# Expert masks of the last stage: from pair products on TensorE to a round trip through DRAM

## The chip, the core and the metric

The kernel runs on one core of a Trainium2 chip. The metric is the device time of one execution in microseconds (us). TensorE is called PE here, VectorE DVE, ScalarE ACT, GpSimd POOL; SP is SyncE, which issues the DMAs of this stage. The time before is 1818.81 us, the median of three runs (1818.36 to 1818.88).

## The reference, cut to what matters

Sixteen sequences of 256 tokens with 256 features go through four layers: cross attention, a mixture of experts, a second cross attention, and a gated linear attention that has a dense and a sparse part. Only the sparse part of the last one is touched:

```
e = softmax(x @ We)                      # 4 experts
_, idx = top_k(e, 1)                     # the first of equal ones
mask = one_hot(idx); rw = e * mask
q_e, k_e = q2 * rw, k2 * rw              # per expert
gk_e = gk2 * mask                        # the decay counts only the expert's own tokens
o_sparse = sum over experts of chunk_gla(q_e, k_e, v, gk_e)
```

Summed over the experts, two tokens s and t meet only if they chose the same expert. Their score is then multiplied by the product of both tokens' gates (the softmax values of their choices), and the decay between them sums the log gates of the tokens of that same expert. So for each sequence a kernel needs, from the choice, a 256 by 256 table of "same expert" (for the decay) and one of "product of the two gates if same expert, else zero" (for the scores), both cut by the causal mask.

## The kernel before

The work is done in stages over the 16 sequences (called batches, b). The change touches only the last stage, stage3_fast, and the code of its first groups, which are run between the last steps of the stage before.

The stage is written out by hand as a sequence of slots p = 0 to 63: batch b = p // 4 and quarter m = p % 4, two of the eight heads in each quarter. Every instruction of PE, DVE, ACT and POOL in the loop is tied to the order of the text, so each engine executes its instructions in the order in which the slots call them. In each slot stand, in this order: start steps, masking of the slot before (masked, second kind, n = 1, which also adds the two masked score blocks on POOL), keys and queries of the next slot (kq), middle steps, rest steps, decays of the next slot (gq with the dense mask, gz with the expert mask em), late steps, the dense score products (sc from f), their masking (at from sc), the factors f, the output of the slot before (o), the second products (sc from q and k). Dictionaries start, middle, rest, late, behind_mask, by_rows and logs say which extra step runs in which quarter; a step with offset 1 works on the next batch.

The extra steps that matter here, by quarter:

- Quarter 0: lows(b+1) makes the low-rank projections of the next batch in one PSUM bank, with the router's logits in rows 81 to 84 of its second half, copied to SBUF by DVE (low) and spread by two small DMAs (lowd, low2). route_rows turns the router's rows into token order by two PE transposes, written into an unused part of the score tile; route_logits takes the maximum of the four logits and the exponentials. outgates(b) begins the output gate, whose logits wait in the tile zs.
- Quarter 1: route_sums and, at the end, route(b+1), which normalises, finds the largest gate and its first expert, and leaves hot: for each token a vector of four with the gate at the chosen expert. norms(b-1) writes 8 KB (rms) to DRAM and reads it back spread over the partitions (r, two DMAs of 256 KB). outgates_end finishes a half of the output gate with a product on POOL (gw).
- Quarter 2: turn_hot turns hot by two PE transposes (hT), turned_hot copies it to SBUF. turn_ahead(b+2) turns 32 by 32 blocks on DVE (tile turned) and moves them by 16 DMAs into xnT, from which quarter 0 of the next batch makes lows(b+2).
- Quarter 3: pairs(b+1) multiplies hT with itself on PE (both): entry s, t is the product of the two gates if the experts are equal and zero otherwise. DVE makes em (both > 0, times dmask) and am (both times amask). steepest takes the largest of the log gates, twice. project(b-1) ends the batch before, with a DMA to the output.

PSUM of this stage: a pool of two banks in turn for all the small products, and single buffers for kq, gq, gz, o and the score tile sc. DMAs are issued by SP alone, which waits in its queue for what a DMA needs. Before the change its DMAs were not tied to the order of the text.

Of the kernel before, what the change touches and what calls it, by code (L numbers as in the profile page):

```python
# [17 lines left out]
P = 128  # L18
# [55 lines left out]
def layers(ctx: ExitStack, tc: tile.TileContext, t, out, check):  # L74
# [1544 lines left out]
    def stage3_fast(early_bank):  # L1619

        with ExitStack() as sx:
# [17 lines left out]
            def transpose(*a):  # L1639
                tc.keep_in_program_order(nc.tensor.transpose(*a))  # L1640

            halves = w1.tile([P, P], F32, tag="halves", name="halves")
            nc.sync.dma_start(out=halves, in_=t["halves"])
# [6 lines left out]

            hots = [w1.tile([P, 2, 4], F32, tag=f"hot{n}", name=f"hot{n}") for n in range(2)]

# [32 lines left out]
            def turn_ahead(b):  # L1685

                xnT[b] = of(b).tile([P, 2, S], F32, tag="xnT", name="xnT")
                y = w1.tile([P, 4, P], F32, tag="turned", name="turned")
                dve3.transpose(y.rearrange("p x d -> p (x d)"), xn[b].rearrange("p k d -> p (k d)"))
                to = xnT[b].rearrange("p k (i s) -> p (k i) s", i=2)  # L1690
                for q in range(0, P, 32):
                    for r in range(0, P, 32):
                        nc.sync.dma_start(out=to[r:r + 32, :, q:q + 32], in_=y[q:q + 32, :, r:r + 32])

            def lows(b):

                low[b] = of(b).tile([P, 2, S], F32, tag="low", name="low")
                ps = bank("low")
                for c in range(2):
                    for k in range(2):  # L1700
                        matmul(ps[:, c * S:(c + 1) * S], la[:, k, c * P:(c + 1) * P], xnT[b][:, k, :],
                                         start=k == 0, stop=k == 1)
                dve3.tensor_copy(low[b][:, 0, :], ps[:, :S])
                dve3.tensor_scalar(low[b][:, 1, :], ps[:, S:], vec[:, V_ONE:V_ONE + 1], None, ALU.add)
                lowd[b] = of(b).tile([P, S], F32, tag="lowd", name="lowd")
                nc.sync.dma_start(out=lowd[b][64:], in_=low[b][:64, 1, :])
                if b > 0:
                    nc.sync.dma_start(out=low2, in_=low[b][64:, 1, P:])

            e_, den_, z_ = {}, {}, {}  # L1710

            def route_rows(b, ps):

                for i in range(2):
                    transpose(ps[:, 64 * i:64 * i + 64], low[b][64:P, 1, tokens(i)], ident[64:P, 64:P])
                z_["rt"] = ps

            def route_logits(b):

                ps = z_.pop("rt")  # L1720
                src = ps.rearrange("p (i e) -> p i e", i=2)[:, :, 17:21]
                mx = st.tile([P, 2], F32, tag="emx", name="emx")
                dve.tensor_reduce(mx, src, AX.X, ALU.max)
                e = e_[b] = st.tile([P, 2, 4], F32, tag="e", name="e")
                dve.tensor_tensor(e, src, bc(mx, [P, 2, 4], 2), ALU.subtract)
                act.activation(e, e, AF.Exp)

            def route_first(b):
                route_rows(b, bank("rt")[:, :P])
                route_logits(b)  # L1730

            def route_sums(b):
                den = den_[b] = st.tile([P, 2], F32, tag="eden", name="eden")
                dve.tensor_reduce(den, e_[b], AX.X, ALU.add)
                dve.reciprocal(den, den)

            def route(b):
                e, shape = e_.pop(b), [P, 2, 4]
                dve.tensor_tensor(e, e, bc(den_.pop(b), shape, 2), ALU.mult)
                m, q, c = (st.tile(x, F32, tag=n, name=n) for n, x in (("em", [P, 2]), ("eq", shape), ("ec", [P, 2])))  # L1740
                dve.tensor_reduce(m, e, AX.X, ALU.max)
                first = bc(prio[:, 4:], shape, 1)
                dve.tensor_tensor(q, e, bc(m, shape, 2), ALU.is_equal)
                dve.tensor_tensor(q, q, first, ALU.mult)
                dve.tensor_reduce(c, q, AX.X, ALU.max)
                dve.tensor_tensor(q, q, bc(c, shape, 2), ALU.is_equal)
                dve.tensor_tensor(hots[b % 2], q, e, ALU.mult)

# [32 lines left out]

            def turn_hot(b):
                ps = bank("hT")
                for i in range(2):
                    transpose(ps[:4, tokens(i)], hots[b % 2][:, i, :], ident)
                z_[b, "hot"] = ps

            def turned_hot(b):
                hT[b] = of(b).tile([4, S], F32, tag="hT", name="hT")
                dve3.tensor_copy(hT[b], z_.pop((b, "hot"))[:4, :S])  # L1790

            def pairs(b):

                x, both = hT.pop(b), bank("both")
                matmul(both[:, 0:S], x[:, :P], x, start=True, stop=True)
                matmul(both[:, S:3 * P], x[:, P:], x[:, P:], start=True, stop=True)
                em[b] = of(b).tile([P, 2, P], F32, tag="em", name="em")
                dve3.scalar_tensor_tensor(em[b], both.rearrange("p (i s) -> p i s", i=2)[:, :, :P], 0.0, dmask,
                                          ALU.is_gt, ALU.mult)
                am[b] = of(b).tile([P, 384], F32, tag="am", name="am")  # L1800
                dve3.tensor_tensor(am[b], both[:, :384], amask, ALU.mult)

# [108 lines left out]
            def products(p, n):  # L1911

                b, m, cols = place(p)
                q, k = fq.pop((p, n)), fk.pop((p, n))
                ps = psa.tile([P, 2, 512], F32, tag="sc", name="sc")
                if n == 0 and m == 0 and b + 1 < B:
                    route_rows(b + 1, ps[:, 1, 384:])
                for lo, hi, i in ((0, S, 0), (P, S, 1)):
                    for j in range(2):
                        r = slice(64 * j, 64 * j + 64)  # L1920
                        matmul(ps[:, j, lo + i * P:hi + i * P], k[r, tokens(i)], q[r, lo:hi],
                                         start=True, stop=True)
                z_[p, n, "sc"] = ps
# [66 lines left out]
            def norms(b):  # L1990
# [8 lines left out]
                act3.activation(y, y, AF.Exp, scale=-0.5)  # L1999
                nc.sync.dma_start(out=rms[b], in_=y[0:P:16, :])  # L2000
                r = z_[b, "r"] = w1.tile([P, 4, S], F32, tag="r", name="r")
                for j in range(2):
                    nc.sync.dma_start(out=r[64 * j:64 * j + 64],
                                      in_=bc(rms[b].rearrange("(m j) s -> j m s", j=2)[j], [64, 4, S], 0))
# [6 lines left out]
            def project(b):  # L2011
                ps = bank("proj")
                for i in range(2):
                    for m in range(4):
# [3 lines left out]
                                               ALU.mult, ALU.add)  # L2018
                nc.sync.dma_start(out=out[b].rearrange("(c p) d -> p c d", p=P), in_=xs[b])

# [3 lines left out]
            def project_part(b, i, h):  # L2024
# [4 lines left out]
                if h == 1:  # L2029
                    dve3.scalar_tensor_tensor(xs[b][:, i, :], pp[i][:, :D], gate[:, 3:4], xs[b][:, i, :],  # L2030
                                              ALU.mult, ALU.add)
                    nc.sync.dma_start(out=out[b, tokens(i)], in_=xs[b][:, i, :])

            def warm():

                ps = bank("warm")
                for _ in range(2):
                    matmul(ps, ones, v[B - 1][:, 0, :], start=True, stop=True)


            start = {3: [(pairs, 1)]}
            middle = {0: [(lows, 1)], 1: [(all_gates, 1)], 2: [(turn_hot, 1)], 3: [(scaled_first, 0)]}

            rest = {0: [(bias, 2)], 1: [(route_sums, 1)], 2: [(turned_hot, 1), (norm_ahead, 2)], 3: [(steepest, 1, 0), (steepest, 1, 1)]}
            late = {1: [(norms, -1)], 2: [(vals, 1), (turn_ahead, 2)], 3: [(project, -1)]}
            behind_mask = {0: [(route_logits, 1)]}
            by_rows = {0: [(outgates, 0)], 1: [(gates_end, 1)]}
            logs = {0: [(outgates_exp, 0, 1, act3.copy), (outgates_end, 0, 0)],
                    1: [(route, 1), (stats, 2), (outgates_end, 0, 1), (gate_logs, 1, 0)],
# [10 lines left out]
            for group in (((bias, 0), (stats, 0)), ((norm, 0),), ((turn, 0),), ((lows, 0),), ((gates, 0, 0),),  # L2060
                          ((gate_logs, 0, 0), (route_first, 0)), ((route_sums, 0), (gates, 0, 1)),
                          ((route, 0), (vals, 0), (gate_logs, 0, 1), (bias, 1))):
# [4 lines left out]
            keys_queries(0)  # L2067
            for f, *a in ((turn_hot, 0), (turned_hot, 0), (stats, 1), (pairs, 0), (norm, 1), (steepest, 0, 0),
                          (steepest, 0, 1)):
                f(*a)  # L2070
# [185 lines left out]
```

## Time and profile before

| what | value |
|---|---|
| median of three runs | 1818.81 us |
| the profiled execution | 1819.15 us |
| its span, first to last instruction | 1817.4 us |
| last stage, from about | 1226 us to the end |
| mean granted TensorE clock | 0.999 |
| matmuls hT from hot, in the loop | 30, 5.7 us busy |
| matmuls both from hT, in the loop | 60, 16.1 us busy |
| transposes of the router's rows, in the loop | 30, 5.0 us busy |

One execution is profiled; its span and what lies around it (1.75 us) make its time. In the lines that follow the numbers ahead of the engine's name are the start and the length in us, counted from the start of the span; a bracket holds the idle time of the engine before the line and who ended it. In a table by stretches each engine has its busy time and its number of instructions, then follow the granted clock, the mean busy share of the 16 DMA engines, and GB/s. Line numbers such as L50 or L1637 are those of helpers through which all instructions of a kind go, so operations are told apart by the names of their tiles. Matmuls are pipelined, and the ends of their lines are modelled.

### The profile page before, as it was taken

What the parts mean: (1) busy time and instruction counts of PE and PEld (TensorE: products, weight loads), DVE (VectorE), ACT (ScalarE), POOL (GpSimd) and SP (SyncE); (2) the same over time, 40 slices, a digit from 0 to 9 for tenths busy, and PEclk for the clock granted to TensorE, in tenths of its full rate; (3) what the DMA queues carried; (4) which work ended last, traced back from release to release, by engine and by line L of the source; (5) the groups of instructions that cost most, each with busy time, mean ns of one, the idle gap of its engine ahead of it and who ended that gap; (6) DMA issues with size and microseconds to landing.
All of it is one profiled execution on the core that took longest, in us unless ns stands there. A gap on an engine that the chain in (4) does not pass through costs nothing.

```text
span 1817.4 us, 35425 instructions
## 1 busy us (share of the span) xinstructions
PE 1787.7 (98%) x13930; PEld 1240.0 (68%) x13930; DVE 1129.3 (62%) x2679; ACT 839.1 (46%) x1743; POOL 1014.9 (56%) x1001
## 2 busy tenths in 40 slices
PE   8999999999999999999999999999999999999997
PEld 5666666666666676666777866657777777777775
DVE  3345656666656666566466378876666666666664
ACT  4433345344443344433343378754554455445542
POOL 3655776567756767557552766414454445444533
PEclk9999999999999999999999999999999999999999
DMA  9800010000010000000058942200111111111110
GB/s 298 240 1 23 16 36 13 28 17 16 31 35 10 29 18 13 27 23 20 10 165 283 233 93 45 35 3 12 26 41 36 29 27 41 36 29 27 41 29 27
DMA packets 110361, 98.05 MB, mean 54 GB/s; under 512 B 43835, under 2 KB 97763, under 8 KB 109673
## 3 DMA queue, kind: packets, MB, share of 16 engines
q1 hardware_dynamic: 97897, 78.91, 14.7%
q0 software_dynamic: 12288, 16.79, 4.6%
q8 instruction: 112, 1.84, 0.4%
q14 instruction: 64, 0.52, 0.1%
HBM read 52.03 MB, written 38.41 MB: 50 GB/s over the span
## 4 chain that ended last, share of the span: by engine, by line
PE 85%; POOL 7%; DVE 4%; ACT 2%; issue 1%; DMA 0%; POOLq 0%; SPq 0%; DVEq 0%; ACTq 0%
PE o L50 11%; PE qk L50 11%; PE v L50 9%; PE sc L50 8%; PE proj L50 7%; PE kq L1637 7%; PE sc L1637 6%; PE gq L1637 4%; POOL es L50 4%; PE ex L50 3%; PE v L1637 3%; PE proj L1637 3%; PE o L1637 3%; POOL rs L50 2%; PE gz L1637 2%; PE low L1637 2%
## 5 line engine op out<-in xcount | busy, mean ns | idle before, releaser
L50 POOL TENSOR_SCALAR rs<-mv 128x2 f32<-128x2 f32 (+2 forms) x85 | 16.2, 190 | 398.3 <-DVE mv L50 388.5
L50 DVE RECIPROCAL rd<-o 128x256 f32<-128x256 f32 x64 | 112.3, 1755 | 164.2 <-PE o L50 123.8
L50 ACT ACTIVATE e<-sc 128x1024 f32<-128x1024 f32 (+1 forms) x192 | 181.5, 1015 | 18.5 <-PE sc L50 18.5
L50 POOL TENSOR_TENSOR at<-at,at 128x768 f32<-128x768 f32 x63 | 114.3, 1815 | 133.8 <-DVE at L50 133.7
L50 PE MATMUL sc<-qk 64*128 64x256 f32 (+1 forms) x1536 | 183.1, 384 | 0.5 <-DVE qk L50 0.5
L50 PE MATMUL o<-e,v 128*32 128x256 f32 (+1 forms) x3072 | 177.9, 379 | 0.0
L50 PEld LDWEIGHTS sc<-qk 64*128 64x128 f32 (+1 forms) x1536 | 132.0, 172 | 55.1 <-issue 26.8
L50 POOL TENSOR_TENSOR esum<-esum,es 128x512 f32<-128x512 f32 x128 | 163.3, 1276 | 10.0
L50 PE MATMUL qk<-kvT,wkv 128*128 128x333 f32 x512 | 164.3, 443 | 0.0
L50 POOL TENSOR_TENSOR es<-e 128x1024 f32<-128x1024 f32 x64 | 151.3, 2365 | 12.0 <-ACT e L50 9.0
L50 ACT ACTIVATE qk<-qk 128x256 f32<-128x256 f32 x128 | 48.7, 380 | 231.9 <-PE qk L50 231.9
L50 POOL TENSOR_TENSOR es<-es,e 77x1024 f32<-77x1024 f32 x64 | 150.3, 2349 | 5.0
L50 PEld LDWEIGHTS o<-e,v 128*32 128x32 f32 (+1 forms) x3072 | 99.9, 110 | 66.3
L50 PE MATMUL qk<-kvT,wq 128*128 128x256 f32 x512 | 134.6, 385 | 0.0
L50 DVE TENSOR_TENSOR at<-sc,amask 128x768 f32<-128x768 f32 x64 | 61.3, 958 | 108.6 <-PE sc L1637 82.5
L50 DVE COPY qk<-qk 128x333 f32<-128x333 f32 x128 | 64.5, 504 | 93.9 <-ACT qk L50 92.8
L50 POOL DMA_INDIRECT x<-rows_out,pos x64 | 101.3, 1582 | 35.9 <-issue 18.0
L50 PEld LDWEIGHTS qk<-kvT,wq 128*128 128x128 f32 x512 | 94.3, 189 | 35.2 <-issue 9.6
L50 PEld LDWEIGHTS qk<-kvT,wkv 128*128 128x128 f32 x512 | 97.2, 190 | 30.0
L50 PE MATMUL proj<-wo0h,oT 128*128 128x256 f32 x512 | 113.7, 380 | 0.3 <-DVE oT L50 0.3
L50 PE MATMUL v<-wkv,kvT 128*128 128x512 f32 x256 | 113.1, 595 | 0.0
L50 PEld LDWEIGHTS proj<-wo0h,oT 128*128 128x128 f32 x512 | 95.9, 190 | 13.9 <-issue 0.8
(268 smaller groups left out, 3914.4 us busy)
## 6 DMA issues: line engine op xcount, KB each, us to landing
rows<-zero SPq DMA_DIRECT2D x16, 640.0 KB
xin<-rows SPq DMA_DIRECT2D x16, 640.0 KB
r<-rms SPq DMA_DIRECT2D x30, 256.0 KB
rows_out<-y SPq DMA_DIRECT2D x16, 384.0 KB
v<-vctx SPq DMA_DIRECT2D x15, 308.0 KB
x<-in_x_dram SPq DMA_DIRECT2D x16, 256.0 KB
rows_out<-y SPq DMA_DIRECT2D x16, 256.0 KB
out_dram<-x SPq DMA_DIRECT2D x15, 256.0 KB
```

Of the source, the lines that this page charges most:

```text
L50: x = getattr(self.engine, name)(*a, **k)
L1637: tc.keep_in_program_order(nc.tensor.matmul(*a, **k))
```

## The change

The choice is no longer carried as a hot vector through PE. Four parts:

- The router's rows are turned on DVE (one transpose of 32 partitions by 256, straight from the PSUM bank of lows into the tile that turn_ahead uses). The small softmax then runs on 32 partitions with 8 by 4 values each, in place of 128 with 2 by 4. route writes the largest gate and a number for its first expert into a 32 by 32 tile, transposes that, and writes 16 rows of it to DRAM (picks: 256 gates and 256 expert numbers).
- Two DMAs read picks back: rows, 512 numbers to every one of the 128 partitions, into a buffer shared with the output gate's zs (with xn for batch 0), and cols, for each partition the gate and the number of its own two tokens, single elements of 4 bytes. same builds em from them by two DVE operations of 128 by 128; weights builds am by four, two for each half.
- The transposes on PE (route_rows, turn_hot), the copy of hT and the pair products are gone. All DMAs of the loop are tied to the order of the text.
- One of the two sums of largest gates (steepest) moves from quarter 3 to quarter 2; the first half of outgates_end moves from the end of quarter 0 to the middle of quarter 1, which puts its POOL product behind the masked sum. For batch 0 em and am are made behind the statistics and both steepest steps, and norm(1) behind them.

```
-            hots = [w1.tile([P, 2, 4], F32, tag=f"hot{n}", name=f"hot{n}") for n in range(2)]
+            choice, chosen = (w1.tile([P, 32], F32, tag=n, name=n) for n in ("choice", "chosen"))
+            nc.gpsimd.memset(choice, 0.0)
...
-                        nc.sync.dma_start(out=to[r:r + 32, :, q:q + 32], in_=y[q:q + 32, :, r:r + 32])
+                        sp.dma_start(out=to[r:r + 32, :, q:q + 32], in_=y[q:q + 32, :, r:r + 32])
...
+                rl[b] = w1.tile([P, 4, P], F32, tag="turned", name="rl")[:, :2, :].rearrange("p x d -> p (x d)")
+                dve3.transpose(rl[b][64:96, :], ps[64:96, S:])
...
-                for i in range(2):
-                    transpose(ps[:, 64 * i:64 * i + 64], low[b][64:P, 1, tokens(i)], ident[64:P, 64:P])
...
+                w, c = choice[own_rows, :8], choice[own_rows, 8:16]
...
+                dve.tensor_reduce(w, e, AX.X, ALU.max)
...
                 dve.tensor_reduce(c, q, AX.X, ALU.max)
-                dve.tensor_tensor(q, q, bc(c, shape, 2), ALU.is_equal)
-                dve.tensor_tensor(hots[b % 2], q, e, ALU.mult)
+                dve.transpose(chosen[own_rows], choice[own_rows])
+                sp.dma_start(out=picks[b].rearrange("n (k a) -> (n k) a", a=32), in_=chosen[64:80])
+                x = w2.tile([P, 512], F32, tag="zs", name="rows") if b else w0.tile([P, 2, D], F32, tag="xn", name="rows")
+                rows[b] = x.rearrange("p (n s) -> p n s", n=2) if b else x
+                sp.dma_start(out=rows[b], in_=bc(picks[b], [P, 2, S], 0))
+                cols_[b] = w1.tile([P, 2, 2], F32, tag="cols", name="cols")
+                sp.dma_start(out=cols_[b], in_=picks[b].rearrange("n (i p) -> p n i", p=P))
...
-                matmul(both[:, 0:S], x[:, :P], x, start=True, stop=True)
-                matmul(both[:, S:3 * P], x[:, P:], x[:, P:], start=True, stop=True)
...
+            def same(b):
+
+                em[b] = of(b).tile([P, 2, P], F32, tag="em", name="em")
                 for i in range(2):
-                    transpose(ps[:4, tokens(i)], hots[b % 2][:, i, :], ident)
...
+                    dve3.scalar_tensor_tensor(em[b][:, i, :], rows[b][:, 1, tokens(i)], cols_[b][:, 1, i:i + 1],
+                                               dmask[:, i, :], ALU.is_equal, ALU.mult)
+
+            def weights(b):
+
+                w, c = (rows[b][:, n, :] for n in range(2))
+                x = am[b] = of(b).tile([P, 384], F32, tag="am", name="am")
+                for i, (lo, hi) in enumerate(((0, S), (S, 3 * P))):
+                    dve3.scalar_tensor_tensor(x[:, lo:hi], c[:, i * P:], cols_[b][:, 1, i:i + 1], w[:, i * P:],
+                                               ALU.is_equal, ALU.mult)
+                    dve3.scalar_tensor_tensor(x[:, lo:hi], x[:, lo:hi], cols_[b][:, 0, i:i + 1], amask[:, lo:hi],
+                                               ALU.mult, ALU.mult)
...
-            start = {3: [(pairs, 1)]}
-            middle = {0: [(lows, 1)], 1: [(all_gates, 1)], 2: [(turn_hot, 1)], 3: [(scaled_first, 0)]}
+            start = {3: [(same, 1)]}
+            middle = {0: [(lows, 1)], 1: [(outgates_end, 0, 0), (all_gates, 1)], 3: [(scaled_first, 0)]}
...
+            rest = {0: [(bias, 2)], 1: [(route_sums, 1)], 2: [(norm_ahead, 2), (steepest, 1, 0)], 3: [(steepest, 1, 1), (weights, 1)]}
...
-            logs = {0: [(outgates_exp, 0, 1, act3.copy), (outgates_end, 0, 0)],
+            logs = {0: [(outgates_exp, 0, 1, act3.copy)],
...
+            for f, *a in ((stats, 1), (steepest, 0, 0), (steepest, 0, 1), (same, 0), (weights, 0), (norm, 1)):
```

## The prediction

> **What bounds the kernel now.** I read the page's engine table first, then the busy time by stretches of the last stage, then its timeline by engine, the DMA queue's own timeline, and the DMA share in half-microsecond stretches.
>
> ```profile
> PE 1787.7 (98%) x13930; PEld 1240.0 (68%) x13930; DVE 1129.3 (62%) x2679; ACT 839.1 (46%) x1743; POOL 1014.9 (56%) x1001
> ...
> core 0: us, PE busy (x) PEld busy (x) DVE busy (x) ACT busy (x) POOL busy (x), PEclk, DMA share, GB/s
> 1570.00:1606.20 36.20, 36.18 (x251) 26.63 (x249) 23.52 (x59) 17.95 (x43) 17.68 (x18) 1.00 0.15 33
> 1606.20:1642.40 36.20, 36.18 (x250) 26.63 (x248) 23.52 (x59) 17.94 (x43) 17.66 (x18) 1.00 0.15 33
> ```
>
> The last stage repeats every 36.2 us (the pairing matmuls start at 1579.36 and again at 1615.60: 36.24), one batch per period, and PE is busy for 36.18 of each, at full granted clock. DVE has 12.7 us free, ACT and POOL 18 each. A PE instruction that goes shortens the period by its start-to-start cost, as long as nothing else is late. Four slots make a period. These pieces of one period show what PE would lose:
>
> ```profile
> 1594.61 0.14 PEld L1640 LDWEIGHTS sc<-ident,low 64*128 64x128 f32 x1 [0.21 <-DVE low L50]
> ...
> 1607.15 1.03 PE L1637 MATMUL kq<-xnT,wq 128*128 128x256 f32 x4
> 1608.02 0.38 PE L1640 MATMUL hT<-ident,hot 128*4 128x128 f32 x2
> 1608.23 0.61 PE L1637 MATMUL gq<-dmask,lg 128*128 128x128 f32 x4
> ...
> 1615.60 0.92 PE L1637 MATMUL both<-hT 4*128 4x256 f32 x4
> 1616.44 1.13 PE L1637 MATMUL kq<-xnT,wk 128*128 128x256 f32 x4
> 1616.55 0.42 DVE L50 SCALAR_TENSOR_TENSOR em<-both,dmask 128x256 f32<-128x256 f32 x1 [0.96 <-PE both L1637]
> 1618.72 0.61 PE L1637 MATMUL gz<-em,lg 128*128 128x128 f32 x4
> ```
>
> The reader should take starts here, not durations: matmuls overlap, and the start of the next group says what one costs. The queue that the new path uses, and the transfer ahead of it:
>
> ```profile
> 1605.21 0.61 SPq L2000 DMA_DIRECT2D rms<-rs  x1
> 1606.96 1.34 SPq L2003 DMA_DIRECT2D r<-rms  x2
> 1611.90 11.56 SPq L1693 DMA_DIRECT2D xnT<-turned  x16
> 1623.63 0.47 SPq L2019 DMA_DIRECT2D out_dram<-x  x1
> ...
> 1608.00:1608.50 0.50, 0.50 (x6) 0.46 (x5) 0.50 (x4) 0.18 (x1) 0.09 (x1) 1.00 0.24 23
> 1610.50:1611.00 0.50, 0.50 (x3) 0.26 (x2) 0.00 (x0) 0.50 (x2) 0.50 (x1) 1.00 0.37 70
> ```
>
> A small write to DRAM (rms) is issued at 1605.21 and its reader at 1606.96: 1.75 us. The 512 KB of r move between about 1608.2 and 1610.9 (DMA share, last column but one). And one pair of lines from the first stage, needed for a rival:
>
> ```profile
> 190.17 2.35 POOL L50 TENSOR_TENSOR es<-es,e 77x1024 f32<-77x1024 f32 x1
> ...
> 191.30 1.25 DVE L50 TENSOR_TENSOR re<-turned,rmx 128x16 f32<-128x16 f32 x1
> ```
>
> **What PE loses.** (a) The pair products: 1615.60 to 1616.44, 0.84 us. (b) The two transposes of the hot rows: in slot 2 the last kq to gq is 1.08 us (1607.15 to 1608.23), in slot 3 without them 0.87 (1581.17 to 1582.04): 0.21. (c) The two transposes of the router's rows: PE stood 0.18 waiting for DVE's low (gz begins at 1593.99 and takes 0.45, the next start is 1594.62). The transposes themselves run partly beside sc matmuls; between 0 and 0.20 (two starts of 0.1) remains for them. I take 0.20 for all of (c), nearest to the wait that is seen, with ends 0.18 and 0.38. Sum 1.25 us a period (1.23 to 1.43), 15 periods: 18.8 us (18.5 to 21.5). The transposes of batch 0 lie in stage 2, where PE is also nearly full (171.55 of 176 us): 0.2 more.
>
> **What DVE gains and loses.** Gone per period: the hT copy 0.40, em 0.43, am 0.55, two small route operations 0.33, 1.7 us in all. New: a 32-partition transpose of 256 columns (row dens<-den, 128x256: 0.44), one of 32x32 (row turned<-rt, 128x64: at most 0.24), two 128x128 products for em (row at<-sc,kden,am: 0.34 each), four for am (2 x 0.47 + 2 x 0.34): about 3.0 us. So +1.3 us on 23.5, in a period of 35. By places: the 0.44 follows low in slot 0 (1594.56) and ends at 1595.0. Queued behind it are the masking, which waits for sc until about 1595.4 anyhow, and, on PE, the bank of low, which the zg matmuls want at about 1595.3: hidden by 0.3 us. The moved sum of largest gates (1.16) runs in slot 2 from about 1609.5 to 1610.7, where the hT copy stood; the next DVE operation, the transpose behind xn, waits for ACT until 1611.13: hidden, by 0.4. In slot 3 DVE no longer waits 0.96 for PE. It runs em (0.5), masking (1.38), u (0.68), one gate sum (1.16), then am. The next thing due is x<-proj at 1621.97 (1622.82 less the 0.84). Counting from 1616.2, am is done at about 1621.5 to 1622.0: hidden, barely; this is the tightest place.
>
> **The output gate behind masking.** POOL did gw at 1600.71 to 1601.97 and then at to 1603.75, for o on PE at 1604.10. The reverse lets at start when DVE is done (1600.08), so it ends near 1601.9, and gw near 1603.2, ahead of k at 1604.10. The matmuls were not stopped there, so I give nothing for it. Without it o would keep 0.35 us of cover. It also frees the buffer that the rows use, long before they are read.
>
> **The DRAM path and what SP queues behind it.** SP's DMAs of this stage already ran in the order of the text (the lines above), so tying them costs nothing; what is new stands between r and the block copies. SP now does rms, r, r, then picks, rows, cols, then the 16 block copies, then the output. The chosen experts are ready at about 1607.3 (route starts at 1606.09, six operations 0.2 apart). SP is free at 1608.30. The write takes 1.75 us if the engines are idle (1610.05); behind r it cannot move before 1610.9, so about 1611.4. Rows issues then (0.65, as one r), moves at +1.25 for 1.1 us (half of r) and lands at 1614.1. Cols issues at 1612.05; its 512 single elements are the unknown price. At the price of a block-copy piece (0.21 share x 0.7 us x 16 engines / 128 pieces = 18 ns) they take 0.6 us of 16 engines; at that of r's 1 KB pieces (2.25 us for 512) 2.25 us. It lands at 1614.9 to 1616.4; I take 1615.1, since its pieces are as short as the block copy's. DVE reaches em at 1615.6, and PE needs em at 1617.87 (1618.72 less 0.84): the landing may be as late as 1617.2. The Trainium skill, DMA: Bandwidth & Descriptors, section Rules for kernel authors, says that a last dimension that isn't contiguous becomes one descriptor per element; by it cols is 512 pieces, and no trace of before shows pieces of 4 bytes.
>
> The block copies start at about 1612.7 in place of 1611.90 (1613.4 at worst), take 11.56, and the last one lands 1.75 after its issue: 1625.4 to 1626.1. The low matmuls read them at 1628.05, in the new time 1627.0 (1.05 of the 1.25 falls before). Hidden by 0.9 to 1.6 us.
>
> **The prologue.** em of batch 0 was ready at 1225.81. Now DVE does x, the statistics and both gate sums (2.33) first, then em: about 1226.4. PE stood 0.7 us before and would stand longer: +0.4 us (between -1, if the 1.05 us of (a) and (b) that go count in full, and +3, if the rows land late).
>
> **Sum.** 1819.15 (the profiled execution: span 1817.4 and 1.75 around it) - 18.8 - 0.2 + 0.4 = 1800.5. The median of the runs, 1818.81, is 0.34 lower; I leave the sum as it stands.
>
> **Rivals.** First, SP's line is late (the other side). SP stands still until picks has landed, with rows, cols and 16 block copies behind. The matmuls of low pay as soon as the line slips 1.6 us past my estimate, and the gain is gone at 1.6 + 1.25 = 2.9 us, that is when the write takes 6 us and not 3.1. For it: it queues behind 512 KB, and DRAM latency is seen only for an idle queue. Against: every row of the queue is at most 1.75 us plus the transfer ahead. With 4 us late, 2.4 us x 14 = 34 less 18.6: 1834.
>
> Second, DVE against POOL. The DVE line at 191.30, 16 elements wide with both inputs in SBUF, ended 0.03 us after POOL's 2.35 us operation did; the same size takes 0.17 elsewhere. The new em and am products have both inputs in SBUF; the old had one in PSUM. em would wait for POOL's u (until 1616.13: in my count), am for at and k (until 1620.65, am done at 1622.0). If also the four products and POOL's alternate badly, DVE is 0.7 us late at x<-proj, and so at masking, where PE has 0.1 us (DVE done 1624.71, sc at about 1624.9): 0.6 x 15 = 9 us, 1809.5. The Trainium skill, SBUF — State Buffer, section Who interferes with whom, says that a DVE instruction with two SBUF inputs and a GpSimd one that reads SBUF shut each other out for a whole instruction; the trace agrees (1.25 us for 16 elements).
>
> Third, the shorter PE line uncovers another engine's chain, such as ACT's exponentials in slot 1 (the weight load of sc waits 0.5 us there for lg, 7.3 us over 15 periods). Against: that chain starts from a PE matmul and moves with it. Half the gain is 9.4: 1810.
>
> **How the numbers follow.** Forecast 0.70 (its own range 1797 to 1804), DVE against POOL 0.11, another chain 0.06, SP's line 0.13 (of which 0.03 costs only the gain). What a measurement tells from no change is 0.2%, 3.6 us. Faster 0.86, same 0.03, slower 0.11. Low 1796.5 is all of (c) and a prologue gain (21.5 + 0.2 + 1 = 22.7); high 1812 takes in the second and third rival, and about 0.15 stays outside.
>
> **What would show it.** Right: periods of 35.0 us with PE still full; no hT, both or router transposes; em on DVE starting before kq of slot 3 and no DVE wait for a DMA longer than 0.5 us; the first block copy about 4.4 us after r's issue ended (1612.7 less 1608.3). Wrong: PE low waiting for a DMA of xnT, PE gz waiting for DVE em, or DVE products of 128x128 longer than 0.6 us with sc waiting for DVE behind them.

## The result, and the profile after

The changed kernel took 1804.08 us, median of four runs (1803.20 to 1804.92), against 1818.85 for the kernel before on the same chip (also the median of four, one of which took 2297.38 and does not count in the ratio): ratio 0.992 (0.990 to 0.9939). The forecast was 1800.5, with a range of 1796.5 to 1812. So the direction was right and the time lies inside the range, but the changed kernel gained 14.8 us where 18.3 were forecast from the median.

The profiled execution took 1804.92 us, with a span of 1803.0. Lines of its page and trace: the engine table, then two stretches of one period each, measured from one write of low to the next (columns as before: busy time of each engine, granted clock, DMA share, GB/s).

```profile
PE 1771.7 (98%) x13802; PEld 1227.0 (68%) x13802; DVE 1168.2 (65%) x2727; ACT 842.4 (47%) x1743; POOL 1018.9 (57%) x1002
...
1551.83:1586.79 34.96, 34.96 (x243) 25.72 (x242) 25.75 (x61) 18.13 (x43) 17.89 (x18) 1.00 0.18 42
1586.79:1621.75 34.96, 34.96 (x243) 25.70 (x242) 25.71 (x61) 18.14 (x43) 17.90 (x18) 1.00 0.17 42
```

PE is still full, and the period went from 36.24 to 34.96 us. That is 1.28 less, where 1.25 was forecast. The queue of SP and the places that the forecast spoke of, in the timeline of the second of these periods:

```profile
1597.21 0.61 SPq L50 DMA_DIRECT2D rms<-rs  x1
1598.95 1.32 SPq L50 DMA_DIRECT2D r<-rms  x2
1600.37 0.55 SPq L50 DMA_DIRECT2D picks<-chosen  x1
1604.81 0.34 SPq L50 DMA_DIRECT2D rows<-picks  x1
1605.20 0.43 SPq L50 DMA_DIRECT2D cols<-picks  x1
1605.73 10.34 SPq L50 DMA_DIRECT2D xnT<-turned  x16
...
1608.33 0.62 DVE L50 SCALAR_TENSOR_TENSOR em<-rows,cols,dmask 128x128 f32<-128x128 f32 x2 [0.97 <-DMA cols<-picks]
1609.64 0.61 PE L1637 MATMUL gz<-em,lg 128*128 128x128 f32 x4
1611.89 0.54 DVE L50 SCALAR_TENSOR_TENSOR am<-rows,cols 128x256 f32<-128x256 f32 x1
1612.10 0.92 POOL L50 TENSOR_TENSOR k<-e,ee 128x256 f32<-128x256 f32 x1
1612.47 0.83 DVE L50 SCALAR_TENSOR_TENSOR am<-am,cols,amask 128x256 f32<-128x256 f32 x1
```

The path through DRAM is just in time. em waits 0.97 us for cols here; its two products are through at about 1608.95, and PE starts gz, which reads em, at 1609.64: 0.7 us remain.

The time came from, and was lost again at, these places (after less before, all between writes of low in the two profiled executions):

| stretch | before | after | difference |
|---|---|---|---|
| start to the write of low of batch 0 | 1204.25 | 1204.49 | +0.24 |
| the opening: to the write of batch 1 | 30.68 | 33.75 | +3.07 |
| to the write of batch 15 | 504.60 | 488.73 | -15.87 |
| from there to the end | 77.87 | 76.03 | -1.84 |
| span | 1817.4 | 1803.0 | -14.4 |

The opening is what went wrong. The granted clock was 1.00 there before (PE busy 2.00 of 2.00 us in each stretch from 1228 to 1234), for example:

```profile
1230.00:1232.00 2.00, 2.00 (x16) 1.49 (x9) 1.66 (x5) 0.50 (x1) 0.23 (x2) 1.00 0.00 0
```

After, in the timeline and then in the table by stretches:

```profile
1222.24 0.38 SPq L50 DMA_DIRECT2D cols<-picks  x1
1225.47 0.61 DVE L50 SCALAR_TENSOR_TENSOR em<-rows,cols,dmask 128x128 f32<-128x128 f32 x2
1225.88 0.75 PE L1637 MATMUL gz<-em,lg 128*128 128x128 f32 x4 [2.26 <-DVE em L50]
1231.96 2.08 PE L1637 MATMUL kq<-xnT,wk 128*128 128x256 f32 x4
...
1228.00:1230.00 2.00, 2.00 (x9) 1.18 (x8) 2.00 (x4) 0.77 (x2) 0.56 (x1) 0.61 0.00 0
1230.00:1232.00 2.00, 2.00 (x13) 0.86 (x13) 0.36 (x1) 0.97 (x2) 0.00 (x0) 0.50 0.04 8
1232.00:1234.00 2.00, 2.00 (x9) 1.64 (x6) 0.79 (x3) 0.00 (x0) 1.00 (x2) 0.50 0.00 0
1234.00:1236.00 2.00, 2.00 (x8) 1.65 (x7) 0.00 (x0) 0.00 (x0) 0.44 (x1) 0.68 0.00 0
1236.00:1238.00 2.00, 2.00 (x15) 1.84 (x13) 0.66 (x2) 0.21 (x1) 0.00 (x0) 1.00 0.00 0
```

PE waits 2.26 us for em of batch 0. Some 2.6 us after that wait the granted clock falls to 0.50 and stays there until about 1235; the group kq<-xnT,wk takes 2.08 us in place of the 1.13 that it takes in the later periods.

### The profile page after: what moved, and what is told of

It reads as the page before. It is cut to its first block, busy times and chain, and to the rows that moved or that the text cites. A ratio compares the mean times of both kernels' runs of the same rounds, so it can differ in the third digit from the quotient of the medians.

```text
span 1803.0 us, 35245 instructions
## 1 busy us (share of the span) xinstructions
PE 1771.7 (98%) x13802; PEld 1227.0 (68%) x13802; DVE 1168.2 (65%) x2727; ACT 842.4 (47%) x1743; POOL 1018.9 (57%) x1002
## 4 chain that ended last, share of the span: by engine, by line
PE 83%; POOL 7%; DVE 5%; issue 1%; ACT 1%; DMA 1%; SPq 0%; POOLq 0%; DVEq 0%; ACTq 0%
PE o L50 12%; PE qk L50 11%; PE v L50 9%; PE sc L50 8%; PE proj L50 7%; PE kq L1637 6%; PE sc L1637 6%; PE gq L1637 4%; POOL es L50 4%; PE o L1637 3%; PE ex L50 3%; PE proj L1637 3%; PE v L1637 3%; PE gz L1637 2%; POOL rs L50 2%; PE low L1637 2%
```

## The experiments

They ran on three chips, on which the kernel before took 1822.57, 1821.08 and 1822.63 us (medians); so ratios are compared, or kernels of one chip. These medians are mixtures. Of the 39 executions of the kernel before on these chips, those with a mean granted clock of 0.999 took 1818.58 to 1820.50 us, those with 0.996 took 1822.70 to 1825.23. The three of the first chip (1818.36 to 1818.88) are like the former, and only one like these was traced; where the others lost clock is not known. So small differences between ratios prove little, and the traces have to decide. The theory to be tested had three parts: the period is PE's and fell by what PE lost; the opening is lost to the clock, after a wait that the landing of cols causes; and the two periods that were longer than the others (35.96 and 35.30) are late landings of cols behind r's transfer. The rivals were DVE's order in the opening, DVE or POOL as the bound, and SP's queue.

**Is the period PE's?** Two matmuls of the shape of the pair products put back in quarter 3; nobody reads their result.

```
 em[b] = of(b).tile([P, 2, P], F32, tag="em", name="em")
+if b > 0:
+    both, x = bank("both"), low[b][:4, 0, :]
+    matmul(both[:, 0:S], x[:, :P], x, start=True, stop=True)
+    matmul(both[:, S:3 * P], x[:, P:], x[:, P:], start=True, stop=True)
```

> The changed kernel with the PE work of the pair products put back: in quarter 3 two matmuls of the same shape (4 rows, 256 and 128 columns), in the same place, on data that lies ready, and with a result that nobody reads. If PE sets the period and the start-to-start cost is the price: 0.84 us a period, 35.8 us, 12.6 us in all, less what the late landings of cols cost before, since em has 0.84 us more cover: +11.3 to +12.6 against the changed kernel. If the period were set by another engine or by the queue, much less.

1816.66 us, against 1805.73 for the changed kernel on the same chip: 10.9 more, a little under the 11.3 to 12.6 expected (ratio to before 0.9977, 0.9968 to 0.9987; the changed kernel there 0.9916, 0.9902 to 0.9929). The usual period is 35.80 us, 0.84 more:

```profile
1615.24 0.92 PE L1637 MATMUL both<-low 4*128 4x256 f32 x4
1616.08 1.13 PE L1637 MATMUL kq<-xnT,wk 128*128 128x256 f32 x4
```

The start-to-start cost of the group, 1616.08 less 1615.24, is the 0.84 that the period grew by. Term (a) is shown. That the remaining 0.44 of 36.24 - 34.96 - 0.84 belongs to (b) and (c), forecast at 0.41 together, is read from PE's starts; no run puts these back.

**What delays the opening: DVE's order or the landing?** em put between the two sums of largest gates.

```
-... (steepest, 0, 0), (steepest, 0, 1), (same, 0), (weights, 0), ...
+... (steepest, 0, 0), (same, 0), (steepest, 0, 1), (weights, 0), ...
```

> One edit against the changed kernel: for batch 0 em is made between the two gate sums and not behind both, so DVE is free for it 1.16 us sooner. The changed kernel takes 1804.1 us (median); there PE stood 2.26 us for this em and then ran at half clock from about 1228.3 to 1235.6 us. If DVE's order made em late: em starts at about 1224.3 in place of 1225.5, PE stands 1.1 us, the clock stays at 1.0, and the time is about 1801. If the landing of cols made it late (in the loop em starts 3.1 us after cols is issued; here cols is issued at 1222.24, so 1225.3): DVE waits for cols instead, em starts within 0.3 us of where it did, and the time stays at 1804 (1803.3 to 1804.8).

1806.83 us, ratio 0.9913 (0.9896 to 0.993): no gain in the time, which says little here because the clock fell once more than in the changed kernel (below). The trace says more. DVE came sooner and then waited itself:

```profile
1224.27 0.38 SPq L50 DMA_DIRECT2D cols<-picks  x1
1227.51 0.61 DVE L50 SCALAR_TENSOR_TENSOR em<-rows,cols,dmask 128x128 f32<-128x128 f32 x2 [1.25 <-DMA cols<-picks]
1227.91 0.75 PE L1637 MATMUL gz<-em,lg 128*128 128x128 f32 x4 [2.25 <-DVE em L50]
```

em began 3.24 us after cols was issued, and 3.23 in the changed kernel, where DVE arrives at the same moment. So the landing sets it, and the second sum, which stands ahead of em in the changed kernel, costs nothing. PE's wait stayed at 2.25 us and the clock fell behind it again.

**Is it the wait or the clock that costs?** Matmuls of 128 by 512 that nobody reads, ahead of batch 0's decays: two, and in another run one.

```
 keys_queries(0)
+fill = bank("fill")
+for _ in range(2):        # range(1) in the second run
+    matmul(fill, ones, v[0][:, 0, :], start=True, stop=True)
 for f, *a in ((stats, 1), (steepest, 0, 0), ...
```

> One edit: two matmuls of 128x512 whose result nobody reads are put on PE ahead of batch 0's first decays, 1.8 us of work in the 2.26 us in which PE waits for em. Nothing that the kernel needs starts sooner. If the lost time of the opening is the clock that follows the wait: the clock stays at 1.0 through 1226 to 1240 us and the time falls by about 2.7 us to 1801.4. If it is only the wait for em: the time stays at 1804 or rises by up to 0.3 us.

> The changed kernel with one 128x512 matmul that nobody reads ahead of batch 0's decays (two took 2.24 us, so one takes about 1.1 and leaves a gap of about 1.1 us ahead of gz). My theory: it is the length of the gap that halves the clock, 2.26 us does and 1.1 does not: clock 1.00 from 1222 to 1240, 30.4 us from the first to the second write of low as with two, 3 to 4 us less than the changed kernel, ratio 0.989 to 0.990. Rival: any idle stretch of over 1 us here is too long: clock 0.5 again for some 6 us, ratio 0.991 to 0.993.

With two 1801.75 us, ratio 0.9888 (0.9871 to 0.9904); with one 1804.33, ratio 0.9906 (0.9888 to 0.9923), both on chips on which the unaltered changed kernel was not run. In the traces, one execution of each, the opening took 30.39 and 30.58 us in place of 33.75, and the clock stayed at 1.00. With two:

```profile
1228.00:1230.00 2.00, 1.53 (x9) 1.02 (x10) 1.97 (x6) 1.22 (x4) 0.80 (x1) 1.00 0.00 0
1230.00:1232.00 2.00, 2.00 (x17) 1.06 (x16) 1.78 (x5) 1.50 (x4) 0.00 (x0) 1.00 0.04 8
```

With one:

```profile
1226.26 0.75 PE L1637 MATMUL gz<-em,lg 128*128 128x128 f32 x4 [1.45 <-DVE em L50]
```

The wait for em is not shortened by the fill, PE only does useless work in it, and yet the 3 us come back: the clock is the cause, not the wait itself. In the traces a wait of 1.45 us here was harmless, and with those of 2.09 us and more half the clock always came, for 6.8 or 10.2 us; in four runs it began while PE still waited, in the others behind the wait. Every trace of the new path without the fill shows the fall, with openings of 33.5 to 36.1 us. The Trainium skill, TensorE: Matmul & The Clock Gate, section What's actually happening, says that the clock halves after an idle window of about 3.4 us; here a wait of 2.26 us was enough, so the measurement decides.

The length of one wait is not a safe measure, however. In the run with em sooner the clock also fell earlier in the opening, behind a wait of only 0.90 us, with one of 0.31 us shortly before it:

```profile
1209.78 3.58 PE L50 MATMUL proj<-wo,oT 128*128 128x256 f32 x8 [0.90 <-DVE oT L50]
1209.96:1213.37 3.41, 3.41 (x12) 2.20 (x15) 2.99 (x2) 1.15 (x4) 0.00 (x0) 0.50 0.02 5
```

PE has these two waits in all 14 traces, the one of before included, and in the other 13 the clock stays at 1.00 behind them. The half-clock stretches of the openings lasted 3.41 us (this one), 6.83 us (five) or 10.24 us (five), whole multiples of 3.41 us, and the two of this run began 20.48 us apart, six times 3.41. So the clock changed in steps of 3.41 us. Laid over the traces as a raster, the eight steps in which PE stood 1.95 us or more were all followed by a fall, none with 1.19 us or less was, and of those between (1.21 to 1.72 us; PE's ends are modelled, so these sums are rough) three were and others were not. How a wait falls on the raster therefore counts beside its length, and that is luck: the 2.26 us of the changed kernel were split over two steps.

The executions that were not traced agree. With two fills all four had a mean clock of 0.997 to 0.999. With one, two took 1802.17 and 1802.55 us at 0.998 and 0.999, and two took 1806.11 and 1806.77 us at 0.995 and 0.996, so one fill does not hold the clock every time.

**Can the landing be had sooner?** First, r's two reads put behind rows and cols (queue: rms, picks, rows, cols, r, r).

```
 sp.dma_start(out=rms[b], in_=y[0:P:16, :])
+def spread(b):            # called behind route, with b - 1
     r = ...
-1: [(route, 1), (stats, 2), ...
+1: [(route, 1), (spread, -1), (stats, 2), ...
```

> One edit: the two DMAs that read r (512 KB) move behind picks, rows and cols in SP's text, so the write of picks has an idle queue ahead of it. If the late landing of cols is 512 KB of r ahead of the write: the write is read 1.75 us after its issue in place of 3.4 to 4.4, em no longer waits for a DMA (8.8 us in total before), the periods of 35.3 and 36.0 us among those of 34.96 go, and the time falls by 0.5 to 1.3 us, to 1802.8 to 1803.6. r lands later, at about 1606 in the period whose u starts at 1605.8: POOL may wait up to 0.5 us, in front of 2 us in which it has nothing to do. If the write is slow by itself: same waits, 1804.

1808.31 us, ratio 0.9921 (0.9899 to 0.9942): no gain. From the issue of picks to that of rows it took 1.36 to 1.40 us in the loop (2.2 in two periods) in place of 3.3 to 4.4, and em no longer waited; but now POOL waited for r, and periods of 35.7 to 35.8 us appeared. The waits of the whole last stage (total, times, longest):

```profile
POOL u L50 <- DMA r<-rms: 26.5, 15, 3.7
```

Then the better order: only the small write goes ahead of r (rms, picks, r, r, rows, cols).

```
 sp.dma_start(out=picks[b]..., in_=chosen[64:80])
+def route_read(b):        # rows, cols
+1: [(route, 1), (spread, -1), (route_read, 1), (stats, 2), ...
```

> One edit: in SP's text the write of picks moves ahead of the two reads of r, and rows and cols stay behind r: rms, picks, r, r, rows, cols. The write meets an idle queue and lands while r is issued. The run with r behind everything took the wait off em but put it on u, which waited 26.5 us for r, with periods of 35.7 us left. If what is late is only whatever comes last in the line, this order leaves neither late: picks lands by r's end of issue, rows is issued about 2.3 us sooner than in the changed kernel, em waits for no DMA, u for less than 2 us in all, all periods 34.96 but the first, and the time falls by 1.3 us against the changed kernel (0.0007). If the long periods come from a slow rms or r (a write that takes 3.4 and not 1.75 us, as in one period of the changed kernel), they stay, and the time is the same within 0.4 us.

1805.97 us, ratio 0.9916 (0.9903 to 0.993); the changed kernel on that chip took 1805.73 with the same ratio. The trace, though, shows the loop cured and the opening worse. From picks to rows it took 1.84 to 2.85 us, em waited for cols nowhere in the loop, and of the 13 later periods 12 are within 0.03 of 34.96, one 35.31. Against the changed kernel on that chip, whose longest period was 36.58, this saves about 2 us. The opening took 34.99 us against 33.49, because the clock fell sooner and for longer (10.24 us, not 6.83). How deep that loss is differs from run to run, and it can hide a gain of this size.

With a fill of one matmul and the keys of batch 0 moved into the wait as well, both gains show:

```
+for m in range(0, 3, 2): ... keys_ahead(0, n, ...)      # from behind decays(0)
+fill = psa.tile([P, 2, 512], F32, tag="sc", name="fill")
+matmul(fill[:, 0, :], ones, v[0][:, 0, :], start=True, stop=True)
 decays(0)
```

> The order of the run with picks first, and the opening mended: the three matmuls for the first keys of batch 0 (k) stand ahead of its decays and not behind them, and one matmul of 128x512 that nobody reads fills most of the rest of the wait for em. Expected by the filling run: the clock stays at 1.0 and some 3.1 us go against the changed kernel; another 0.5 to 1.0 us because k no longer follows em; 0 to 1.3 us from the order. Together 3.6 to 5.4 us below the changed kernel, ratio to before about 0.9895.

1800.78 us (1799.84 to 1800.95), ratio 0.9888 (0.9873 to 0.9903), the fastest version here: about 5 us below the changed kernel on the same chip (1804.10 to 1807.51). Its opening took 30.15 us at a clock of 1.00.

**How near is SP's line to the edge?** picks copied a second time through DRAM.

```
-sp.dma_start(out=picks[b]..., in_=chosen[64:80])
+sp.dma_start(out=first[b]..., in_=chosen[64:80])
+sp.dma_start(out=picks[b]..., in_=first[b]...)
```

> One edit: picks is written to one place in DRAM, copied from there to a second, and read from the second: one more trip in SP's line, some 2 us, ahead of rows, cols and the 16 block copies. It measures what cover is left. In the changed kernel em ends 0.7 us before gz needs it, and has waited 0.97 us for cols: so 2 us more should stop PE for about 1.3 us in each of 14 periods, 1804 + 18 = 1822, slower than before the change. The prediction's count (2.1 us of cover from the estimate of the landing to the point where PE pays, of which the landing as measured has used about 1.4) says the same to within 0.5 us a period. The rival, that the landing is well covered and the two long periods come from elsewhere: 1804 to 1808.

1826.65 us, ratio 1.0025 (1.0013 to 1.0037), slower than before the change. Waits of the last stage:

```profile
DVE em L50 <- DMA cols<-picks: 38.4, 15, 4.0
...
PE gz L1637 <- DVE em L50: 12.2, 15, 4.1
```

em waited 2.6 us at the mean, where it was 0.7 in the changed kernel, and PE waited for em in the opening and in all later periods but one. One more short DMA on this path takes away the whole gain. The first rival was real; the change stops short of it by less than 1 us.

**The parts that were forecast at nothing.** Three runs undo one of them each: the output gate ahead of masking again, both sums of largest gates in quarter 3 again, and SP's DMAs not tied.

```
-1: [(outgates_end, 0, 0), (all_gates, 1)]       # e9: back into quarter 0's logs
-2: [(norm_ahead, 2), (steepest, 1, 0)]          # e10: back into quarter 3
-sp = Pinned(tc, nc.sync)                        # e11
+sp = nc.sync
```

> The changed kernel, with the output gate of the first slot ahead of masking's second product on POOL again, as in the kernel before. My theory: in the changed kernel POOL does at (1592.53 to 1594.34), gw (to 1595.58), and k at 1596.09 after 0.51 us of waiting for ACT, so the order of the two does not reach PE: ratio to the kernel before as the changed kernel's, 0.991 to 0.993, periods 34.96 us. Rival: o on PE has no cover left (it had about 0.35 us before) and waits for the later at: up to 0.9 us a period, 12 us, ratio 0.998.

> The changed kernel, with both sums of largest gates in slot 3 again, as in the kernel before. My theory: DVE runs without a gap from em to the next masking there (em 1608.33, x<-proj 1613.87, masking 1614.68), so 1.21 us more makes masking 1.2 us late, PE's sc had about 0.1 us of cover: periods of 35.5 to 36.1, 8 to 16 us more than the changed kernel, sc on PE waiting for DVE at every time. Rival: DVE catches up before PE needs it (it has 2.08 us free ahead of the next low): periods 34.96, no change.

> The changed kernel, with SP's DMAs of the last stage not tied to the order of the text. My theory: they ran in that order in the kernel before too, so nothing changes: ratio 0.991 to 0.993, within 1 us of the changed kernel. Rival: without the tie another order of picks, r and the block copies comes out, and waits of em for cols (8 to 12 us in all in the changed kernel) go or grow by more than 5 us.

They took 1809.61, 1813.90 and 1812.02 us, with ratios of 0.9928 (0.9914 to 0.9941), 0.9956 (0.9939 to 0.9972) and 0.994 (0.9927 to 0.9954); the changed kernel had 0.9916 and 0.992 on two other chips. These intervals overlap or touch, so the periods have to decide. The usual one is 35.13, 35.23 and 35.22 us against 34.96: about 0.17, 0.27 and 0.26 more, a loss of 2.4 to 3.8 us over 14 periods; untied, four are 36.0 to 36.8 long, where the changed kernel has one of 35.96. None of the three parts was free. I compared PE's starts, group by group from the write of low, with those of the changed kernel, in a usual period of each. In the first, everything agrees up to the output products of the first slot, o, which start 0.17 later; the weight loads show why:

```profile
1599.89 0.63 PEld L1637 LDWEIGHTS o<-at,v 128*64 128x64 f32 x8 [0.29 <-POOL at L50]
```

In the other two the first differences are 0.17 at the sc products of the last slot and 0.27 at den behind them. With both sums back, PE's wait there is for masking:

```profile
1586.96 0.73 PEld L1637 LDWEIGHTS sc<-q,k 64*128 64x128 f32 x8 [0.41 <-DVE at L50]
```

Untied, a block copy slipped in ahead of the reads. SP stood there until DVE had made the tile turned, and rows was issued 4.84 us after picks, 3.3 to 4.4 in the changed kernel:

```profile
1606.89 0.55 SPq L1745 DMA_DIRECT2D picks<-chosen  x1
1610.59 0.64 SPq L1695 DMA_DIRECT2D xnT<-turned  x1
1611.73 0.34 SPq L1748 DMA_DIRECT2D rows<-picks  x1
1612.12 0.42 SPq L1750 DMA_DIRECT2D cols<-picks  x1
```

em waited 24.1 us for cols in all, against 8.8 in the first run of the changed kernel and 11.9 in its second. DVE then came late to the same masking as with the sums.

## Why the prediction was right, and where it was wrong

- **What bounds it, and (a), (b), (c).** Right. 1.25 us a period was forecast and 1.28 measured; the pair products are 0.84 by the trace and by putting them back. (b) is 0.21: kq to gq in quarter 2 takes 0.87 now, 1.08 before. (c) fell from gz to o by 2.46 - 2.26 = 0.20, the value taken.
- **The prologue.** This is the step that failed: "+0.4 us" was worked out, with a range of up to +3, and the opening took 3.07 longer. The prediction put em's start down to DVE's order. In fact cols' landing sets it, 3.2 us after its issue, as moving em showed. It then counted PE's wait as lost time at one price. PE's wait lasted 2.26 us, and its larger cost was the clock behind it: with PE kept busy the opening took 30.4 us, 0.3 less than before the change. That 3.07 lies near the range's upper end is luck: +3 was given for a late landing, which by the runs with the fill cost nothing by itself.
- **The DRAM path.** Right that it fits, wrong in the write's size. "About 1611.4", 3.1 us from the issue of picks to that of rows, is 3.3 to 4.4 in the trace. In the period shown, cols' issue to em took 3.13 us, against 3.05 by the price of a short piece (1612.05 to 1615.1). So the block copies began 5.5 us after r's issue ended, not 4.4, em waited 0.97 and not under 0.5, and it started 0.96 us behind kq of slot 3 (1607.37), not before it. None of this reached PE in the usual period. In one period it did: the write of rms took 3.36 us from issue to its reader (1526.29 to 1529.65) in place of 1.75, picks and cols followed late, and em waited 2.18. That period took 35.96 us; the section on the hardware shows what stood in the way.
- **The sum.** From the profiled execution 18.6 us were forecast and 14.2 came. The opening accounts for 2.9 of the missing 4.4 (3.07 less the 0.2 of its forecast, 0.4 - 0.2), the period of 35.96 for 1.0, and one of 35.30 for 0.3. The comparison is with an execution of the kernel before that kept its clock; one of those at 0.996 would have left a larger gain. The 35.30 is there in nearly every run of the new path, the one without waits for cols too; what makes it I have not found.
- **DVE against POOL.** The mechanism was there and the price small. am's products took 0.54 and 0.83 us where POOL's k, 0.92 in place of 0.73, ran beside them, against 0.48 each in the opening. In the usual period PE did not wait for masking; in five places it did, 3.4 us in all (before in two, 1.4 us). The Trainium skill, SBUF — State Buffer, section Who interferes with whom, says that a DVE instruction with two SBUF inputs contends with a GpSimd one that reads SBUF; these rows agree in that all three operations got longer. They were not shut out for their whole length, as the forecast had it: 0.48, 0.73 and 0.48 us make 1.69, and the three were through in 1.41 (1611.89 to 1613.30).
- **The moved gate sum, the output gate and the queue's order.** "I give nothing for it" and "tying them costs nothing" are right as costs but miss what the parts do. Each keeps 0.17 to 0.27 us a period that the shorter PE line would otherwise lose to POOL, DVE or SP. The cover of 0.35 us that o was said to keep was counted in the old period. In the run with the gate back, POOL's at ended 9.41 us after the write of low (9.16 before the change), while o would start at 9.30 (9.51 before).
- **DVE's margin in slot 3.** "hidden, barely; this is the tightest place" was right, although DVE's busy time rose by 2.2 us a period (23.52 to 25.71) and not by 1.3. My later expectation for the sums put back, 0.5 to 1.1 us a period, was too high: 0.27. With the sums later, am no longer ran beside POOL's k (0.47 and 0.48 us), and part of the delay was taken up by slack ahead of masking.

## What to carry to other kernels

When a full engine's line gets shorter, every part that was hidden with a few tenths to spare has to be counted again in the new period; parts that look like tidying up (a product moved, a queue tied) can be what makes the gain arrive. A wait of TensorE is not priced by its length alone: look at the granted clock in the microseconds behind it, in more than one execution, and put work into the wait if it falls. Of a small transfer on a queue, send the write whose landing starts a chain ahead of the large reads, and let the reads of the chain go behind them.

## What the hardware showed that was not expected

- PE waits of 2.1 us and more at the head of this stage came with a granted clock of 0.5 for 6.8 or 10.2 us, at the cost of some 3 us or more; one of 1.45 us did not in the trace, and one of 0.90 us did in one trace of 14. The half-clock stretches there were 3.41, 6.83 or 10.24 us long.
- A read of 512 pieces of 4 bytes was issued in 0.38 to 0.44 us in the changed kernel, and where em waited for it, em began 3.1 to 3.5 us after the issue began.
- A small write to DRAM took 1.36 to 1.40 us from issue to its reader's issue with nothing before it on the queue but another small write (2.2 in two periods), 1.84 to 1.89 in most periods with r's reads issued behind it, and 3.3 to 4.4 behind r's 512 KB.
- A load of code seems to have delayed a small write. The write of rms, eight pieces of 1 KB, took 3.36 us to its reader once in the changed kernel (1526.29 to 1529.65), 1.72 to 1.78 in the other 14 periods, and 1.72 to 1.77 in all 15 of the kernel before. The transfers from 1526 to 1530 in the changed kernel, 40 slices of 0.1 us, then packets, MB and share by queue:

```profile
GB/s 0 0 0 0 0 0 0 0 0 0 0 0 0 0 0 236 0 0 0 0 0 0 0 0 10 0 0 0 0 0 0 0 0 0 0 0 0 0 0 0
...
q8 instruction: 1, 0.02, 1.5%
q1 hardware_dynamic: 16, 0.01, 0.7%
```

The stretch from 1597 to 1601, with a usual write, has no instruction packet, and its write moves whole in two neighbouring slices:

```profile
GB/s 0 0 0 0 0 0 0 0 0 0 0 0 0 0 61 21 0 0 0 0 0 0 0 0 0 0 0 0 0 0 0 0 0 0 113 184 236 287 307 369
```

In the late case 23.6 KB move in one slice, a block of code with most of the write, and 1 KB, one piece of the write, comes 0.9 us later. In the packets of the trace the block, 16 KB, begins at 1527.51 and takes 0.98 us; seven pieces of the write start from 1527.53 to 1527.60, the eighth at 1528.49, as the block ends. All 13 traces of the new path have exactly one write of rms with such a late piece, and each time it starts within 0.02 us of the end of a block. It is in the same batch in 12 of them; with the pair products kept, whose PE has more instructions, it is four batches later. So where the code load falls goes with the program. Two blocks that overlapped a write held no piece of it (the run with the pair products kept, at 1641.48, and the run with the gate back, at 1493.99), so overlap alone is not enough. No run moves the load alone; that it is the cause is read from these coincidences.
